# 1/sigma of a leaving chunk: from GpSimd's power to ScalarE's logarithm and exponential

## The chip, the cores and the metric

The kernel runs on one core of a Trainium2 chip. The metric is the device time of one execution in microseconds (us). A core has five engines with a queue each: TensorE (PE; its weight loads are shown apart as PEld), VectorE (DVE), ScalarE (ACT), GpSimd (POOL) and SyncE (SP), which here only issues transfers. SBUF is the memory on the core, PSUM the small memory that TensorE writes and that VectorE and ScalarE can read.

## The reference

Two layers on an image batch x of shape 8 x 128 x 128 x 128 (image, height, width, channel). Layer 0 is linear attention with a norm and a residual. Layer 1 is a selective scan over each image in four directions. What the change touches is the end of layer 1, for all 8 x 16384 tokens of 256 inner channels:

```python
y = (y0 + y1 + y2 + y3).transpose(0, 2, 1)      # the four scans' sums, one row a token
zf = jax.nn.silu(z.reshape(Bb, L, Cd))
yz = y * zf
mu = yz.mean(-1, keepdims=True)
xc = yz - mu
var = (xc * xc).mean(-1, keepdims=True)
yn = gamma * xc / jnp.sqrt(var + 1e-05) + beta
out = yn @ Wout
```

and each scan, for the step t of a direction, with the decay dA = exp(delta * A) and delta a softplus:

```python
xc = dA * xc + dut[..., None] * Bt[:, :, None, :]
y = jnp.einsum('kbcn,kbn->kbc', xc, Ct)
```

## The kernel before

The program has three stages one after the other: layer 0, the front of layer 1 (projection, 3x3 convolution, silu, and what the scans need, written to DRAM), and the scans with the end of layer 1 (`layer1_scan`). The change lies in the third, which begins at about 4436 us of the profiled execution.

The third stage holds y for one image in SBUF, as two tiles of 128 channels by 16384 positions. It goes through 8 output images o, four scans (slots) each, and every scan in 16 chunks of 1024 positions: 512 units, one in each call of `step(n)`. A chunk of a scan, for each half c of the channels:

- `load` (L923) and `load_rows` (L916, L917) bring the inputs through SP's queue; `delta` (L934, TensorE) and `soften` (L938, ScalarE's softplus into tile sp) make delta one step ahead;
- `decay` (L942, ScalarE) makes the decays with Exp, in PSUM (tile px);
- `weigh` (L951, GpSimd) multiplies sp with the input ubt into h, one of two buffers in turn;
- `scan` (L959 forward, L961 backward, VectorE) runs the recurrence over h, starting from the last column of the h of the chunk before;
- `emit` (L979, L982, L989 or L993, VectorE) multiplies with C, which `spread` (L967, TensorE) laid out; for the first slot of an image it writes y itself, for the others `gather` (L1001, VectorE) and `add` (L1009, GpSimd) add to y.

Softplus and Exp need different activation tables, so each step has two ACT_TABLE_LOADs, put there by the compiler ahead of the first activation that needs one.

When an image's four scans are done, its 16 chunks *leave* during the first 16 steps of the next image (for the last image, in 16 steps after all scans): `leaving[n]` is the chunk of step n. In `step`, `now` is the chunk that leaves in this step, `last` the one of the step before, `soon` the next. For a chunk m:

- `gate` (L1029) multiplies y with silu(z) into z: one half on GpSimd a step earlier, the other on VectorE; `square` (L1032, ScalarE) puts the squares into y;
- `moments` (L1042, TensorE) makes the mean and the mean of squares, `keep` (L1048, ScalarE) copies them, `to_tokens` (L1054, TensorE) turns them, `square_mean` (L1058, ScalarE, tile mv), `variance` (L1062, VectorE): rstd = mean of squares minus squared mean, 128 x 8 numbers, at the end of the step;
- `deviation` (L1066, L1067, GpSimd), one step later, between the two weighings: 1/sigma as (max(var, 0) + 1e-5) to the power -0.5, the exponents taken from the tile `half2`;
- `project` (L1074, TensorE) applies Wout, and `store` (L1080, VectorE), one step later between the two scans, multiplies with 1/sigma, adds a constant row and sends the tile r (two buffers) to DRAM.

`add_d` (L907, a DMA issue of GpSimd that adds the D term into y) stands at the end of some steps around an image's change, `fetch` (SP) brings z.

`in_order` ties every instruction of an engine to the one written before it on the same engine. So the order in `step` is the order of each queue; the engines run apart as far as their data lets them. `deviation(last[1])` stands after `weigh(n, 0)` in the text, hence in GpSimd's queue between the two weighings:

```python
        if last:
            deviation(last[1])
        if live:
            weigh(n, 1)
```

Of the kernel before, what the change touches and what calls it, by code (L numbers as in the profile page):

```python
# [8 lines left out]
F32 = mybir.dt.float32  # L9
BF16 = mybir.dt.bfloat16  # L10
AF = mybir.ActivationFunctionType
ALU = mybir.AluOpType
# [4 lines left out]
P = 128  # L17
# [7 lines left out]
GW = 4  # L25
# [9 lines left out]
EPS1 = 1e-5  # L35
# [712 lines left out]
def layer1_scan(ctx: ExitStack, tc, ubs, xps, zs, gs, dtw, dtb, a_log, gamma, beta, w_out, out):  # L748
# [15 lines left out]
    nc = tc.nc  # L764
    const = ctx.enter_context(tc.tile_pool(name="l2c", bufs=1))
# [31 lines left out]


    NR = R + 2
    half = const.tile([P, GW, 2], F32, name="half2")  # L800
    nc.vector.memset(half, -0.5)
    rws, dws = [], []
    for i in range(3):
        t = const.tile([P, CH], BF16, name=f"rows{i}")
# [104 lines left out]
    def load_rows(n):  # L909
        sl, i = units[n]  # L910
        m = sl.at(i)
        rw = rws[n % 3]
        md = NCH - 1 - m if sl.dt_turned_back else m
        src = xps[sl.dt_image, sl.dt_order].rearrange("j r l -> (j r) l")
        for j in range(3):
            nc.sync.dma_start(rw[3 * NR * j : 3 * NR * j + 3 * NR, :], src[:, md * CH : md * CH + CH])  # L916
        nc.sync.dma_start(rw[96:99, :], xps[sl.b, sl.order, :, R + 1, m * CH : m * CH + CH])  # L917

    def load(n, c):
        sl, i = units[n]  # L920
        m = sl.at(i)
        ubt[n, c] = wp.tile([P, CH], F32, name="ubt", tag="ub", bufs=4)
        nc.sync.dma_start(ubt[n, c], ubs[sl.b, sl.order, c][:, m * CH : m * CH + CH])  # L923
# [16 lines left out]
    def decay(n, c):  # L940
        sl, i = units[n]
        nc.scalar.activation(da[n, c], sp[n, c], AF.Exp, scale=sa[:, sl.s, c : c + 1])  # L942

    def weigh(n, c):
        if c == 0:
            hs[n] = wp.tile([P, NC2, CH], F32, name="h", bufs=2)
        u, t, h = ubt.pop((n, c)), sp.pop((n, c)), hs[n][:, c, :]
        if units[n][0].permuted:
            u = u.rearrange("p (e h w) -> p h e w", e=2, w=W // 2)
            t, h = (v.rearrange("p (h e w) -> p h e w", e=2, w=W // 2) for v in (t, h))  # L950
        nc.gpsimd.tensor_tensor(h, u, t, ALU.mult)  # L951

    def scan(n, c):
        sl, i = units[n]
        x, e = da[n, c], hs[n][:, c, :]
        last = 0 if sl.back else CH - 1
        start = 0.0 if i == 0 else hs[n - 1][:, c, last : last + 1]
        if sl.back:
            nc.vector.tensor_tensor_scan(e[:, ::-1], x[:, ::-1], e[:, ::-1], start, ALU.mult, ALU.add)  # L959
        else:  # L960
            nc.vector.tensor_tensor_scan(e, x, e, start, ALU.mult, ALU.add)  # L961
# [7 lines left out]
    def emit(n, hf):  # L969

        sl, i = units[n]
        h = hs[n][:, :, hf * 512 : hf * 512 + 512]
        c = cps.pop((n, hf)).to_broadcast([P, NC2, GN])
        if sl.place == 0:
            v = sl.y_at(i, hf)
            split = "p c (a b) -> p c a b"
            nc.vector.tensor_tensor(v, h.rearrange(split, b=H), c.rearrange(split, b=H), ALU.mult)  # L979
            return  # L980
        if hf != sl.first:
            nc.vector.tensor_tensor(h, h, c, ALU.mult)  # L982
            return
        p = da.pop((n, 1))
        if sl.y_turned:
            ts[n] = p.rearrange("p (c b a) -> p c b a", c=NC2, a=GW)
            t = p.rearrange("p (c b a) -> p c a b", c=NC2, a=GW)
            split = "p c (a b) -> p c a b"
            nc.vector.tensor_tensor(t, h.rearrange(split, b=H), c.rearrange(split, b=H), ALU.mult)  # L989
        else:  # L990
            t = p.rearrange("p (c q) -> p c q", c=NC2)
            ts[n] = t.rearrange("p c (a b) -> p c a b", b=H)
            nc.vector.tensor_tensor(t, h, c, ALU.mult)  # L993

    def gather(n):

        sl, i = units[n]
        v = sl.y_at(i, sl.first)
        if sl.y_turned:
            v = v.rearrange("p c a b -> p c b a")  # L1000
        nc.vector.tensor_tensor(v, v, ts.pop(n), ALU.add)  # L1001
# [15 lines left out]
    def mirrored(o, m, hf):  # L1017
        p = 2 * m + hf
        return 2 * NCH - 1 - p if o % 2 == 1 else p

    def fetch(o, m):
        for hf in range(2):
            zt[m, hf] = z = wp.tile([P, NC2, GN], F32, name="z", bufs=6)
            p = mirrored(o, m, hf)
            nc.sync.dma_start(z, zs[o].rearrange("c p l -> p c l")[:, :, p * GN : p * GN + GN])

    def gate(o, m, hf, eng):
        z, ym = zt[m, hf], piece(m, hf)
        eng.tensor_tensor(z, ym[:, :, ::-1] if o % 2 == 1 else ym, z, ALU.mult)  # L1029

    def square(m, hf):
        nc.scalar.activation(piece(m, hf), zt[m, hf], AF.Square)  # L1032

    def moments(m):

        pm = pe.tile([P, GN], F32, name="pm", tag="pt")
        for c in range(NC2):
            for j in range(2):
                for hf in range(2):
                    at = 32 * (2 * j + hf)  # L1040
                    v = piece(m, hf) if j else zt[m, hf]
                    nc.tensor.matmul(pm[at : at + 32, :], mean, v[:, c, :], start=(c == 0), stop=(c == NC2 - 1))  # L1042
        pts[m, "rows"] = pm
# [16 lines left out]
    def variance(m):  # L1060
        rst[m] = rstd = sm.tile([P, GW, NC2], F32, name="rstd")
        nc.vector.tensor_tensor(rstd, pts.pop(m)[:, :, :, 1], mv.pop(m), ALU.subtract)  # L1062

    def deviation(m):
        rstd = rst[m]
        nc.gpsimd.tensor_scalar(rstd, rstd, 0.0, EPS1, ALU.max, ALU.add)  # L1066
        nc.gpsimd.tensor_tensor(rstd, rstd, half, ALU.pow)  # L1067

    def project(m, hf, bank):
        z = zt.pop((m, hf))  # L1070
# [36 lines left out]
    def step(n):  # L1107
        live = 0 <= n < N
        then = n + 1 < N
        before = 1 <= n <= N  # L1110
        now, last, soon, later = (leaving.get(n + i) for i in (0, -1, 1, 2))
        first = before and units[n - 1][0].place == 0
        if before:
            half1 = units[n - 1][0].first
            emit(n - 1, half1)
            if not first:
                gather(n - 1)
        if now and last:
            gate(*now, 1, nc.vector)
        if before:  # L1120
            emit(n - 1, 1 - half1)
        if n + 2 < N:
            load_rows(n + 2)
        if n in fetched:
            fetch(*fetched[n])
        if live:
            decay(n, 0)
        if now:
            square(now[1], 1)
        if live:  # L1130
            decay(n, 1)
            weigh(n, 0)
            if n + 2 < N:
                load(n + 2, 0)
        if last:
            deviation(last[1])
        if live:
            weigh(n, 1)
            if n + 2 < N:
                load(n + 2, 1)  # L1140
        if now:
            moments(now[1])
        if live:
            scan(n, 0)
            da.pop((n, 0))
        if last:
            for hf in range(2):
                store(*last, hf)
        if then:
            for c in range(NC2):  # L1150
                delta(n + 1, c)
        if now:
            keep(now[1])
        if then:
            soften(n + 1, 0)
        if now:
            to_tokens(now[1])
            square_mean(now[1])
        if then:
            soften(n + 1, 1)  # L1160
        if live:
            scan(n, 1)
        if first:
            hs.pop(n - 1)
        if now:
            variance(now[1])
        if live:
            half1 = units[n][0].first
            spread(n, half1, "pc")
            spread(n, 1 - half1, "pt")  # L1170
        if soon and now:
            gate(*soon, 0, nc.gpsimd)
        elif soon:
            gate(*soon, 1, nc.gpsimd)
        elif later:
            gate(*later, 0, nc.gpsimd)
        if soon:
            square(soon[1], 0)
        if now:
            p = da.pop((n, 1)) if live else px.tile([P, CH], F32, name="px")  # L1180
            for hf in range(2):
                project(now[1], hf, p[:, hf * 512 : hf * 512 + 512])
        elif live and units[n][0].place == 0:
            da.pop((n, 1))
        if before and not first:
            add(n - 1)
            hs.pop(n - 1)
        if n in weighed:
            units[weighed[n]][0].weights()
        if n in summed:  # L1190
            add_d(*summed[n])
# [78 lines left out]
```

## Time and profile before

| | |
|---|---|
| median of 3 runs | 9188.95 us (9188.0 to 9196.81) |
| profiled execution, its own time | 9184.71 us |
| its span, first to last instruction | 9182.9 us |
| mean granted TensorE clock | 0.797 |
| GpSimd: clamp L1066, 128 x | 143.7 us, mean 1123 ns |
| GpSimd: power L1067, 128 x | 212.6 us, mean 1661 ns |
| GpSimd: weighing L951, 1024 x | 2420.9 us, mean 2397 ns |
| VectorE: gate L1029, 120 x | 261.3 us, mean 2177 ns |
| VectorE: variance L1062, 128 x | 18.1 us, mean 142 ns |
| ScalarE: table loads at L938 and L942, 512 x each | 656.9 us each, mean 1283 ns |
| ScalarE: square of the mean L1058, 128 x | 22.6 us, mean 177 ns |

Of the profile, the page gives the busy time of each engine in 40 slices of the span, as digits in tenths; a timeline lists one engine's instructions with start and length in us from the span's start, and in brackets the idle time before an instruction with the work that seems to have ended it; `x2` joins equal neighbours. A waits view lists who waited for whom. Recorded lengths include time in which an instruction had started and could not go on.

### The profile page before, as it was taken

To read this page: it belongs to the slowest core of one execution; us is meant where nothing else is said; L and a number is where in the kernel's file an instruction comes from. 1 tells how busy PE (TensorE), PEld (TensorE's weight loads), DVE (VectorE), ACT (ScalarE), POOL (GpSimd) and SP (SyncE) were. 2 spreads that over 40 slices of the span, in tenths; PEclk is the share of its full clock that TensorE was granted. 3 is DMA by queue.
4 is the path that set the end of the run, shared out by engine and by line. 5 is a ranking of instruction groups with operands and counts; after the bars stand their busy time and mean duration, and the time that the engine had idled before them with its cause. 6 is when DMAs were issued, how large, how long until landed. Compare 5 with 4: busy or idle time off the path is not lost. (4 is left out here: it accounts for less than half of the span.)

```text
span 9182.9 us, 91090 instructions
## 1 busy us (share of the span) xinstructions
PE 6273.2 (68%) x24350; PEld 3080.2 (34%) x24512; DVE 7929.7 (86%) x7889; ACT 7102.3 (77%) x8066; POOL 7317.2 (80%) x4684
## 2 busy tenths in 40 slices
PE   8999999998899999999334536345363463643636
PEld 5556555564333333333102304023041130311403
DVE  6667666673899999999799999999999999999996
ACT  5565665568799999999687887888888878788885
POOL 3446544465689988888599898998999989999897
PEclk9999999999999999999556758557575575755857
DMA  1322333313488888888659668586685876958767
GB/s 77 147 103 86 136 117 147 147 54 150 167 244 252 249 246 245 242 245 242 197 161 245 195 194 249 155 246 205 188 258 154 233 213 179 259 162 219 231 175 213
DMA packets 934769, 1750.66 MB, mean 191 GB/s; under 512 B 150228, under 2 KB 376148, under 8 KB 926064
## 3 DMA queue, kind: packets, MB, share of 16 engines
q1 hardware_dynamic: 873328, 1509.92, 49.9%
q0 software_dynamic: 60928, 234.90, 13.9%
q8 instruction: 200, 3.28, 0.1%
q14 instruction: 313, 2.56, 0.1%
HBM read 1052.36 MB, written 692.12 MB: 190 GB/s over the span
## 5 line engine op out<-in xcount | busy, mean ns | idle before, releaser
L951 POOL TENSOR_TENSOR h<-ubt,sp 128x1024 f32<-128x1024 f32 x1024 | 2420.9, 2397 | 342.5 <-ACT mv L1058 118.1
L934 PE MATMUL px<-rows,dtw 128*128 128x512 bf16 x1893 | 909.9, 573 | 2302.7 <-DVE y L1001 1084.5
L534 DVE SCALAR_TENSOR_TENSOR acc<-xb,cw,acc 128x1024 f32<-128x1024 f32 x1024 | 1320.5, 1290 | 133.0 <-ACT xb L502 89.5
L526 POOL TENSOR_TENSOR tap<-tap 128x1024 f32<-128x1024 f32 x512 | 1223.2, 2392 | 245.3 <-ACT tap L524 221.6
L938 ACT ACTIVATE sp<-px 128x1024 f32<-128x1024 f32 x1024 | 1046.6, 1023 | 435.6 <-PE px L934 391.4
L934 PEld LDWEIGHTS <-dtw 128*128 128x128 bf16 x2048 | 168.8, 110 | 3093.0 <-issue 1027.2
L961 DVE TENSOR_TENSOR_SCAN h<-px,h 128x1024 f32<-128x1024 f32 x512 | 1177.5, 2332 | 32.3 <-ACT px L942 15.9
L959 DVE TENSOR_TENSOR_SCAN h<-px,h 128x1024 f32<-128x1024 f32 x512 | 1178.0, 2331 | 21.0 <-POOL h L951 18.7
L1009 POOL TENSOR_TENSOR y<-y,h 128x512 f32<-128x512 f32 x768 | 1162.8, 1561 | 3.0 <-DVE h L982 3.0
L942 ACT ACTIVATE px<-sp,sa 128x1024 f32<-128x1024 f32 x1024 | 1110.4, 1109 | 6.1
L515 PE MATMUL acc<-xi,wt 128*128 128x512 f32 x2048 | 938.6, 601 | 53.7 <-ACT ures L539 53.5
L524 ACT ACTIVATE tap<-xb,cw 128x1024 f32<-128x1024 f32 x768 | 837.4, 1139 | 15.0 <-POOL xb L499 14.8
L282 POOL TENSOR_TENSOR q<-q,qs 128x512 f32<-128x512 f32 x256 | 273.0, 1066 | 694.6 <-DVE qs L281 691.1
L938 ACT ACT_TABLE_LOAD x512 | 656.9, 1283 | 169.5 <-PE px L934 122.8
L942 ACT ACT_TABLE_LOAD x512 | 656.9, 1283 | 9.2
L1074 PEld LDWEIGHTS px<-wg,z 128*128 128x128 f32 x4096 | 566.4, 222 | 114.9 <-issue 109.1
L967 PE MATMUL pc<-rows,csel 128*128 128x512 bf16 x1017 | 515.4, 588 | 85.1 <-DVE rstd L1062 76.2
L515 PEld LDWEIGHTS acc<-xi,wt 128*128 128x128 f32 x2048 | 375.9, 190 | 573.9 <-issue 412.9
L1074 PE MATMUL px<-wg,z 128*128 128x128 f32 x4096 | 565.5, 305 | 0.0
L488 PE MATMUL pxb<-xi,wi 128*128 128x512 f32 x1024 | 496.3, 607 | 2.1 <-ACT xb L497 2.1
L1001 DVE TENSOR_TENSOR y<-y,px 128x1024 f32<-128x1024 f32 x384 | 468.6, 1220 | 14.4
L982 DVE TENSOR_TENSOR h<-h,pc 128x1024 f32<-128x1024 f32 x384 | 466.0, 1214 | 0.0
(152 smaller groups left out, 14653.6 us busy)
## 6 DMA issues: line engine op xcount, KB each, us to landing
ubt<-ubs SPq DMA_DIRECT2D x1024, 512.0 KB
zs<-z SPq DMA_DIRECT2D x512, 256.0 KB
ubs<-ures SPq DMA_DIRECT2D x256, 512.0 KB
ubs<-turned SPq DMA_DIRECT2D x256, 512.0 KB
z<-zs SPq DMA_DIRECT2D x256, 512.0 KB
y<-gs POOLq DMA_DIRECT2D x128, 1024.0 KB, 10.2
gs<-du POOLq DMA_DIRECT2D x96, 1024.0 KB, 8.8
rows<-xps SPq DMA_DIRECT2D x1536, 60.0 KB
```

The costliest lines, as they stand in the source:

```text
L515: nc.tensor.matmul(acc[:, s, :], wt[:, j, c, :], x, start=(j == 0), stop=(j == len(ON_PE) - 1))
L524: nc.scalar.activation(t, at(n, c, *d), AF.Copy, scale=weight(n, c, *d))
L526: nc.gpsimd.tensor_tensor(sums[n, c], sums[n, c], t, ALU.add)
L534: nc.vector.scalar_tensor_tensor(acc, at(n, c, *d), weight(n, c, *d), acc, ALU.mult, ALU.add)
L934: nc.tensor.matmul(p[:, hf * 512 : hf * 512 + 512], sl.dw[:, c * P : c * P + P], src, start=True, stop=True)
L938: nc.scalar.activation(t, da[n, c], AF.Softplus)
L942: nc.scalar.activation(da[n, c], sp[n, c], AF.Exp, scale=sa[:, sl.s, c : c + 1])
L951: nc.gpsimd.tensor_tensor(h, u, t, ALU.mult)
L959: nc.vector.tensor_tensor_scan(e[:, ::-1], x[:, ::-1], e[:, ::-1], start, ALU.mult, ALU.add)
L961: nc.vector.tensor_tensor_scan(e, x, e, start, ALU.mult, ALU.add)
L1009: nc.gpsimd.tensor_tensor(v[:, c], v[:, c], h[:, c], ALU.add)
L1074: nc.tensor.matmul(po[:, w, :], z[:, c, w * H : w * H + H], wg[:, c, :], start=(c == 0), stop=(c == NC2 - 1))
```

## The change

1/sigma is made in three instructions on two other engines. VectorE clamps the variance and adds epsilon right behind `variance`, at the end of the step in which the chunk leaves. ScalarE takes the logarithm and then exp(-0.5 x) of it in the next step, after both decays and the square, ahead of the weighing in the text. GpSimd's two instructions go, and the tile of exponents `half2` with its memset. At the head of such a step, before the first decay, the activation table set `natural_log_exp_and_others` is asked for by name: a set that serves both Ln and Exp, so that the decays' Exp and the two new activations can run from it.

```diff
     NR = R + 2
-    half = const.tile([P, GW, 2], F32, name="half2")
-    nc.vector.memset(half, -0.5)
...
     def variance(m):
         rst[m] = rstd = sm.tile([P, GW, NC2], F32, name="rstd")
         nc.vector.tensor_tensor(rstd, pts.pop(m)[:, :, :, 1], mv.pop(m), ALU.subtract)
+        nc.vector.tensor_scalar(rstd, rstd, 0.0, EPS1, ALU.max, ALU.add)

     def deviation(m):
         rstd = rst[m]
-        nc.gpsimd.tensor_scalar(rstd, rstd, 0.0, EPS1, ALU.max, ALU.add)
-        nc.gpsimd.tensor_tensor(rstd, rstd, half, ALU.pow)
+        nc.scalar.activation(rstd, rstd, AF.Ln)
+        nc.scalar.activation(rstd, rstd, AF.Exp, scale=-0.5)
...
         if n in fetched:
             fetch(*fetched[n])
+        if last:
+            nc.scalar.preload_act_table_set("natural_log_exp_and_others")
         if live:
             decay(n, 0)
         if now:
             square(now[1], 1)
         if live:
             decay(n, 1)
+        if last:
+            deviation(last[1])
+        if live:
             weigh(n, 0)
             if n + 2 < N:
                 load(n + 2, 0)
-        if last:
-            deviation(last[1])
         if live:
             weigh(n, 1)
             if n + 2 < N:
```

## The prediction

> **What bounds the kernel now.** I read the page first, then the timeline of one engine at a time over one step of the scans, then the waits, then single lines where two engines meet.
>
> The page says that from slice 17 on VectorE and GpSimd are both almost full, and ScalarE is not:
>
> ```profile
> PE 6273.2 (68%) x24350; PEld 3080.2 (34%) x24512; DVE 7929.7 (86%) x7889; ACT 7102.3 (77%) x8066; POOL 7317.2 (80%) x4684
> ...
> DVE  6667666673899999999799999999999999999996
> ACT  5565665568799999999687887888888878788885
> POOL 3446544465689988888599898998999989999897
> ```
>
> That share doesn't say what GpSimd's part is worth where the change acts: in the 128 steps in which a chunk leaves. Three timelines (start, length, engine, line) of one such step, from one variance (L1062) to the next 11.28 us later, show it.
>
> ```profile
> 5064.44 0.13 DVE L1062 TENSOR_TENSOR rstd<-pq,mv 128x8 f32<-128x8 f32 x1
> 5064.62 1.22 DVE L979 TENSOR_TENSOR y<-h,pc 128x1024 f32<-128x1024 f32 x1
> 5065.76 2.34 DVE L1029 TENSOR_TENSOR z<-y,z 128x1024 f32<-128x1024 f32 x1
> 5068.02 1.21 DVE L979 TENSOR_TENSOR y<-h,pc 128x1024 f32<-128x1024 f32 x1
> 5069.15 2.34 DVE L959 TENSOR_TENSOR_SCAN h<-px,h 128x1024 f32<-128x1024 f32 x1
> ```
>
> ```profile
> 5064.65 2.37 POOL L951 TENSOR_TENSOR h<-ubt,sp 128x1024 f32<-128x1024 f32 x1 [1.33 <-ACT mv L1058]
> 5066.98 1.23 POOL L1066 TENSOR_SCALAR rstd<-rstd 128x8 f32<-128x8 f32 x1
> 5068.29 1.66 POOL L1067 TENSOR_TENSOR rstd<-rstd,half 128x8 f32<-128x8 f32 x1
> 5069.91 2.37 POOL L951 TENSOR_TENSOR h<-ubt,sp 128x1024 f32<-128x1024 f32 x1
> ```
>
> ```profile
> 5066.06 1.28 ACT L942 ACT_TABLE_LOAD   x1
> 5067.35 1.12 ACT L942 ACTIVATE px<-sp,sa 128x1024 f32<-128x1024 f32 x1
> 5068.41 1.04 ACT L1032 ACTIVATE y<-z 128x1024 f32<-128x1024 f32 x1
> 5069.35 1.10 ACT L942 ACTIVATE px<-sp,sa 128x1024 f32<-128x1024 f32 x1
> 5071.44 0.58 ACT L1048 COPY sr<-pm 128x512 f32<-128x512 f32 x1 [0.99 <-PE pm L1042]
> ```
>
> See three things. First, GpSimd sits idle 1.33 us before its first weighing (L951); that starts 0.14 us after the second scan (L959, 5062.18 + 2.33) ends, because the new h goes into a buffer that this scan still reads. The name L1058 in the bracket can't be the cause, it ended 0.7 us earlier. Second, VectorE's gate (L1029) takes 2.34 us here and 1.22 us at the end of the program, where GpSimd is idle:
>
> ```profile
> 9065.93 1.22 DVE L1029 TENSOR_TENSOR z<-y,z 128x1024 f32<-128x1024 f32 x1
> ```
>
> It does not run at half speed: it stands until the weighing ends (5064.65 + 2.37 = 5067.02) and needs 1.08 us from there. GpSimd's small clamp (L1066), queued behind the weighing, ends only with the gate. The two engines exclude one another, and a whole GpSimd instruction has to finish first. Third, the step is a closed chain: weighing 0.21 us after the variance starts, 2.37, gate 1.08, then by start times L979 1.05, scan 2.26, store (L1080) 2.05, scan 2.26; together 11.28. The deviation (L1066, L1067) is not in it.
>
> **The change part by part.** *GpSimd loses* L1066 and L1067: 143.7 + 212.6 = 356 us over 128 steps. They are off the chain above, so in an ordinary step their removal is worth nothing. What hides them is the idle 1.33 us and the fact that the second weighing, ended at 5072.3, is wanted only at 5073.46; it will start about 1.8 us earlier and GpSimd will only idle longer.
>
> *ScalarE gains* a logarithm and an exponential on 128x8. The nearest rows are 177 ns (L1058) and 208 ns (L778); with some 0.1 us between dependent ones, 0.5 us a step. They stand after the second decay (ends 5070.45) and before L1048, where ScalarE waits 0.99 us for TensorE. They'd be done at about 5071.0, the store needs 1/sigma at 5071.41. Cost 0, with 0.4 us of cover; if that were gone the store would pay the overrun. The clamp is long finished by then.
>
> *The table.* The load before L942 stays one load; it only names a set with both functions, and Square and Copy run under every table in this trace. Softplus takes it away again as now. Cost 0. The row gives 1.28 us for a load and the next activation follows at once (5066.06 to 5067.35), so two loads too many would take 2.6 us of ScalarE a step. The Trainium skill, "ScalarE: Activation LUTs", section "What ACT_TABLE_LOAD costs", adds a drain of 1.38 us to each switch, 2.66 us in all. By that page two loads too many would be 5.3 us, an estimate; the row has no such drain. In the last 16 steps, where no scan runs, the load may be repeated 16 times: 1.28 us inside ScalarE's pauses before the second Square; 0 to 4 us in all, I take 0.
>
> *VectorE gains* the clamp, 128x8 from and to SBUF. Bare, it is near L210 (214 ns) or L1062 (132 to 167 ns). Even 0.2 us on VectorE is hidden in an ordinary step, since the gate behind it waits 1.26 us for the weighing anyway. What counts is who gets in first, because this form also waits for GpSimd. The only row of the same shape shows it: the clamp-like L779 stood 1.00 us until a GpSimd fill was over.
>
> ```profile
> 4436.51 1.00 DVE L779 TENSOR_SCALAR sa<-sa 128x8 f32<-128x8 f32 x1
> ```
>
> ```profile
> 4436.09 1.40 POOL L805 MEMSET rows<- 128x1024 bf16 x1
> ```
>
> The Trainium skill speaks against the change here: "GPSIMD Engine Reference", section "8. Key points", says that GpSimd shares its SBUF interfaces with VectorE, which collides in a two-port mode or with two SBUF inputs. By that page alone, as an estimate, each of the 112 clamps beside a scan could be made to wait.
>
> Who waits is settled by start times. In an ordinary step the weighing starts 0.208 to 0.226 us after the variance does. The clamp depends on the variance's end (0.132) and dependent VectorE instructions follow 35 ns after the one before (L210, L212 and L281 show 34 to 36 ns idle), so it starts at 0.167, some 42 ns ahead. The closest meetings in the trace: a copy that started with a GpSimd product (333.62) won and delayed it by 0.6 us; a copy 42 ns behind one (910.84 against 910.80) lost and took 1.56.
>
> ```profile
> 333.62 0.73 DVE L152 COPY v<-x 128x512 f32<-128x512 f32 x1
> ```
>
> ```profile
> 910.84 1.56 DVE L152 COPY v<-x 128x512 f32<-128x512 f32 x1
> ```
>
> So I take it that the clamp wins, with 0 to 0.06 us delay for the weighing (gates let GpSimd go about 0.13 us before their recorded end; the clamp's end at 0.3 to 0.38 then gives 0.17 to 0.25 against 0.21).
>
> I went through all 112 variances that lie beside scans. 93 are ordinary: 93 x 0.02 = +2 us (0 to 6).
>
> 12 are late: the variance waited for ScalarE's L1058 by about 0.55 us after a store held by its buffer, and the weighing was already running. There the clamp stands to its end, L979 follows, the second weighing, no longer behind the deviation, enters before the gate, and the gate waits again. At 5613.91: weighing ends 1.94 after the variance, second 4.30, gate 5.39, next variance 13.0 instead of 11.26: +1.76. Twelve make 21 us; but VectorE's waits for the store buffer in these stretches are 20.1 us, and a delay just before such a wait is taken out of it. The late ones come in runs with these waits between them, so I keep 9 us (0 to 21).
>
> 7 are the first of an image, with GpSimd in an add (L1009). Where it lasts 1.5 to 2.1 us more (5 cases) the clamp waits it out and the weighing passes the gate, but the scan's wait of 1.13 us for the late weighing goes: +1.27 each. In the other 2, +0.1. Sum +6.6 us. Against it, GpSimd was late in the step after (add, deviation and DMA issue L907 in one step: 12.3 us, five times, and 11.7 twice, against 11.28); without the deviation it isn't: 5 x 1.03 + 2 x 0.39 = -5.9 us. L907's issue moves up some 2 to 3 us, as do the loads of ubt on SP's queue that wait for the second weighing; nothing is queued behind them that VectorE misses.
>
> The end (16 steps of 7.34 us, TensorE products and ScalarE copies in turn): the clamp delays the gate by 0.2 us against about 1 us of cover. 0. The removed memset, once, is 0.06 us before the loop.
>
> Sum: 2 + 9 + 6.6 - 5.9 = +11.7 us on the profiled execution (9184.71, its span 9182.9); that execution lies 4.24 us under the median 9188.95. I predict 9188.95 + 11, about 9200.
>
> **The rivals.** *The weighing wins* (slower). If the clamp starts only some 50 to 85 ns later than reckoned, each ordinary step goes like a late one: weighing ends 2.57, L979, second weighing 4.92, gate 6.0, next variance 13.63: +2.35, 93 times, 219 us, with the rest about 9420. For it: the margin is 42 ns, and after a scan L979 follows only at 0.105 us, as it waits for two things. Against: the clamp waits for one.
>
> *The second weighing passes the gate* even when the clamp won, being ready at once: about +2.3 us a step, 9425. Against it: wherever a waiting VectorE instruction met the end of a GpSimd one, it got in, as the gate above did.
>
> *Relief* (faster). The seven stretches of leaving chunks have 37 us beyond 15 steps of 11.28 each, mostly store waits. If an earlier L907 and earlier loads untangle the transfers and the late steps vanish, up to -37: some 9160. Against: the amount of data is the same.
>
> *The merging fails:* a load for the decays and one for the logarithm; first decay 1.28 later, 1/sigma at about 5073.4 instead of 5071.41: +2.0 x 112, 9413. Nothing in the profile speaks for it but that the trace has no such set.
>
> **How the numbers follow.** Likeliest case 0.57, its own range 9180 to 9220 (terms at their ends, and 10 us for shifted transfers); weighing wins 0.20; second weighing 0.05; relief 0.13; tables 0.04; the remaining 0.01 slower. This kernel can be told from no change at about 0.2%, 18 us. Inside the likeliest, 0.39 fall within that and 0.18 above. Faster 0.13; same 0.39; slower 0.18 + 0.20 + 0.05 + 0.04 + 0.01 = 0.48. To leave out no more than 2 in 10 the range must reach the lost race: 9165 to 9440, which leaves out about half of relief and the far ends.
>
> **What would show it.** Right: clamps of 0.13 to 0.3 us in 93 steps, steps of 11.3 us, GpSimd's idle before L951 up by some 2.9 us, clamps near 2 us in the late and first steps, 1024 loads before L938 and L942 or in their place plus at most 16. Wrong: clamps of 2.4 us everywhere with steps of 13.6; store waits gone; more loads. The whole stands on 35 ns between dependent VectorE instructions and on start times being the order of entry.

## The result, and the profile after

| | before | after |
|---|---|---|
| median, side by side | 9193.18 us (9188.0 to 9198.33, 6 runs) | 9229.87 us (9218.37 to 9244.15, 6 runs) |
| ratio | | 1.0042, 95% interval 1.0029 to 1.0054 |
| profiled execution, its span | 9182.9 us | 9242.3 us |

The changed kernel is slower by 37 us, 0.4%. The forecast was 9200 us, +11. Its times also spread over 26 us where those of before spread over 10, and the execution that was profiled is the slowest of its six (9244.15 us). Of the experiments' executions two, of `e5` and `e6`, ran at 11954 and 14046 us with a granted clock of 0.54 and 0.56; they are slow ones and left out of the ratios.

The line of busy time and the costliest group on GpSimd, from the page of the changed kernel. Line numbers have moved by one to two: L949 is the weighing, L1060 the variance, L1061 the new clamp, L977 emit, L1027 the gate, L1079 the store.

```profile
PE 6335.4 (69%) x24512; PEld 3079.4 (33%) x24512; DVE 8013.9 (87%) x8016; ACT 7168.9 (78%) x8338; POOL 7063.2 (76%) x4428
...
L949 POOL TENSOR_TENSOR h<-ubt,sp 128x1024 f32<-128x1024 f32 x1024 | 2485.5, 2465 | 620.2 <-ACT mv L1056 320.2
```

GpSimd lost 254 us of busy time. That is less than the 356 us of its two instructions, because records include waiting: those of the weighing grew by 65 us (2485.5 against 2420.9) and those of its gates by 29. It stands idle before the weighing for 620 us instead of 343. VectorE gained 84 us. The groups of VectorE by line (busy us, mean ns of one, idle before) show where:

```profile
L1061 DVE TENSOR_SCALAR rstd<-rstd 128x8 f32<-128x8 f32 x128 | 95.4, 746 | 4.4
L1060 DVE TENSOR_TENSOR rstd<-pq,mv 128x8 f32<-128x8 f32 x128 | 18.6, 146 | 30.6 <-ACT mv L1056 29.7
```

The variance before it, of the same shape, takes 146 ns; the clamp 746 on average. The view of this one line says that the average describes none of them (shortest, median and longest, in ns):

```profile
L1061 DVE TENSOR_SCALAR rstd<-rstd x128: 171/172/2357, 4980.4 to 9233.6; 128x8 f32<-128x8 f32 x128
```

**An ordinary step** goes as forecast. VectorE's timeline of the changed kernel, and GpSimd's for the same stretch:

```profile
8685.15 0.13 DVE L1060 TENSOR_TENSOR rstd<-pq,mv 128x8 f32<-128x8 f32 x1
8685.32 0.17 DVE L1061 TENSOR_SCALAR rstd<-rstd 128x8 f32<-128x8 f32 x1
8685.40 1.21 DVE L977 TENSOR_TENSOR y<-h,pc 128x1024 f32<-128x1024 f32 x1
8686.53 2.28 DVE L1027 TENSOR_TENSOR z<-y,z 128x1024 f32<-128x1024 f32 x1
```

```profile
8685.36 5.69 POOL L949 TENSOR_TENSOR h<-ubt,sp 128x1024 f32<-128x1024 f32 x2 [3.27 <-ACT mv L1056]
8691.01 2.36 POOL L1027 TENSOR_TENSOR z<-y,z 128x1024 f32<-128x1024 f32 x1
```

The clamp starts 0.17 us after the variance, 0.04 us ahead of the weighing, and is done in 0.17 us. GpSimd was idle for 3.27 us instead of 1.33; the prediction had put the rise at 2.9, and the rest of it stands in the record of the second weighing, which waits for the gate. The next variance comes at 8696.43, 11.28 us later. (`x2` joins the two weighings; VectorE's gate gets in between them.)

**A lost step** of the same image, 90 us earlier:

```profile
8594.75 0.17 DVE L1060 TENSOR_TENSOR rstd<-pq,mv 128x8 f32<-128x8 f32 x1
8594.96 2.21 DVE L1061 TENSOR_SCALAR rstd<-rstd 128x8 f32<-128x8 f32 x1
8597.08 1.21 DVE L977 TENSOR_TENSOR y<-h,pc 128x1024 f32<-128x1024 f32 x1
8598.22 2.33 DVE L1027 TENSOR_TENSOR z<-y,z 128x1024 f32<-128x1024 f32 x1
...
8608.38 0.17 DVE L1060 TENSOR_TENSOR rstd<-pq,mv 128x8 f32<-128x8 f32 x1
```

```profile
8594.78 4.67 POOL L949 TENSOR_TENSOR h<-ubt,sp 128x1024 f32<-128x1024 f32 x2 [5.61 <-ACT mv L1056]
8599.43 3.35 POOL L1027 TENSOR_TENSOR z<-y,z 128x1024 f32<-128x1024 f32 x1
```

The weighing starts 0.18 us ahead of the clamp. The clamp stands until it ends (8597.14), both weighings run back to back (4.67 us instead of 5.69), the gate waits for the second, and the next variance comes after 13.63 us. This is the course that the rival "the weighing wins" worked out, and it occurs in some steps only. That the length agrees to the hundredth is in part chance: the gate ends 5.80 us after the variance, not 6.0, and the next variance starts about as much later, since it waits for the mean (below).

Which steps? The lengths of the clamps of all 112 chunks that leave beside scans, read off the trace, show it: in the first and the seventh image the first eleven clamps are blocked (2.16 to 2.36 us), in the other five images the first one and one or two more, 34 in all. So most of the profiled execution's loss sits in two images. From an image's first variance to its sixteenth, beyond 15 steps of 11.28 us, in us:

| image | 1 | 2 | 3 | 4 | 5 | 6 | 7 | sum |
|---|---|---|---|---|---|---|---|---|
| before | 5.2 | 7.2 | 3.4 | 5.5 | 9.6 | 4.8 | 1.2 | 36.9 |
| after | 25.6 | 8.5 | 4.9 | 5.2 | 9.6 | 10.7 | 25.5 | 90.0 |

These stretches hold 53 of the 59 us by which the two spans differ, and images 1 and 7 alone 45. Some 4 us lie between the stretches and 3 in the last 16 steps.

**Why a run of lost steps keeps itself going.** TensorE's timeline in the lost step, then the same products in the ordinary step:

```profile
8595.19 3.73 PE L1073 MATMUL px<-wg,z 128*128 128x128 f32 x32
8601.82 1.07 PE L1040 MATMUL pm<-z,mean 128*32 128x512 f32 x2 [2.90 <-DVE y L977]
```

```profile
8690.08 0.62 PE L1040 MATMUL pm<-z,mean 128*32 128x512 f32 x2 [0.80 <-DVE y L977]
```

As emit and gate are late, TensorE pauses 2.90 us before the moments instead of 0.80, and then makes them at 1.07 us each instead of 0.62. The table by stretches (us, busy time of PE, PEld, DVE, ACT, POOL, then the granted clock, DMA share, GB/s) shows why:

```profile
8598.11:8601.51 3.40, 0.81 (x8) 0.62 (x6) 3.40 (x3) 1.83 (x2) 3.40 (x2) 1.00 0.73 211
8601.52:8604.92 3.40, 3.10 (x16) 1.02 (x16) 3.40 (x7) 1.46 (x4) 1.26 (x1) 0.50 0.90 310
8604.94:8615.16 10.22, 6.48 (x50) 5.12 (x46) 10.05 (x11) 8.21 (x10) 6.78 (x3) 1.00 0.57 172
8615.18:8618.58 3.40, 3.16 (x16) 1.01 (x16) 3.40 (x7) 1.40 (x4) 1.19 (x1) 0.50 1.00 320
```

In the interval with the pause TensorE is busy for 0.81 of 3.40 us; in the next one its granted clock is one half, and that one holds most of the moments. ScalarE's copy and softplus come later for it, and the square of the mean with them:

```profile
8608.17 0.17 ACT L1056 ACTIVATE mv<-pq 128x8 f32<-128x8 f32 x1
```

It starts at 8608.17 and ends at 8608.34, the last scan is over at 8608.24, and the next variance (8608.38) cannot start with the scan's end. In the ordinary step the same square is over 0.53 us before its variance (8685.15):

```profile
8684.44 0.18 ACT L1056 ACTIVATE mv<-pq 128x8 f32<-128x8 f32 x1 [0.48 <-PE pq L1052]
```

GpSimd's weighing doesn't need the mean, starts on time, and is first again. A variance that waits for the mean takes 0.17 us instead of 0.13, so the clamp is late by that too: it starts 0.20 us behind it, not 0.17. The five traces in which the clamp is on VectorE in SBUF and the mean is made at the same place (the changed kernel twice, `e4`, `e5`, `e10`) bear this out. First steps and steps with an added copy left aside, 92 clamps were blocked, and each of their variances began within 0.06 us of the end of the square of the mean; of the 426 that were not blocked, one did. Of the 91 steps examined (the first 13 of each image), the moments fall on a half-speed interval in 27: the first step of each image, as before the change, and the 20 steps that follow it in images 1 and 7 (in each the ten after the first).

### The profile page after: what moved, and what is told of

It is laid out like the page before. It is cut to its first block, busy times and chain, and to the rows that moved or that the text cites. A ratio compares the mean times of both kernels' runs of the same rounds, so it can differ in the third digit from the quotient of the medians.

```text
span 9242.3 us, 91051 instructions
## 1 busy us (share of the span) xinstructions
PE 6335.4 (69%) x24512; PEld 3079.4 (33%) x24512; DVE 8013.9 (87%) x8016; ACT 7168.9 (78%) x8338; POOL 7063.2 (76%) x4428
## 5 line engine op out<-in xcount | busy, mean ns | idle before, releaser
L949 POOL TENSOR_TENSOR h<-ubt,sp 128x1024 f32<-128x1024 f32 x1024 | 2485.5, 2465 | 620.2 <-ACT mv L1056 320.2
L932 PE MATMUL px<-rows,dtw 128*128 128x512 bf16 x2048 | 951.9, 564 | 2244.5 <-DVE y L999 1081.0
L936 ACT ACTIVATE sp<-px 128x1024 f32<-128x1024 f32 x1024 | 1047.2, 1024 | 434.0 <-PE px L932 413.6
L1007 POOL TENSOR_TENSOR y<-y,h 128x512 f32<-128x512 f32 x768 | 1159.2, 1556 | 4.8 <-DVE h L980 4.8
L940 ACT ACTIVATE px<-sp,sa 128x1024 f32<-128x1024 f32 x1024 | 1110.5, 1109 | 6.1
```

Of the source, the lines that this page charges most:

```text
L932: nc.tensor.matmul(p[:, hf * 512 : hf * 512 + 512], sl.dw[:, c * P : c * P + P], src, start=True, stop=True)
L936: nc.scalar.activation(t, da[n, c], AF.Softplus)
L1007: nc.gpsimd.tensor_tensor(v[:, c], v[:, c], h[:, c], ALU.add)
```

## The experiments

My theory from these traces: the ordinary step is won as predicted, the loss comes from clamps that lose their entry, and one loss makes the next. Rivals: ScalarE's part or its table costs something; GpSimd's earlier work disturbs the transfers. In the diffs lines are against the changed kernel where nothing else is said. Ratios stand against the kernel before on the same chip.

**Take the blocking away: the clamp reads PSUM.** The variance is written back to its PSUM tile.

```diff
-        nc.vector.tensor_tensor(rstd, pts.pop(m)[:, :, :, 1], mv.pop(m), ALU.subtract)
-        nc.vector.tensor_scalar(rstd, rstd, 0.0, EPS1, ALU.max, ALU.add)
+        v = pts.pop(m)[:, :, :, 1]
+        nc.vector.tensor_tensor(v, v, mv.pop(m), ALU.subtract)
+        nc.vector.tensor_scalar(rstd, v, 0.0, EPS1, ALU.max, ALU.add)
```

> The changed kernel, but the variance is written back into its PSUM tile and the clamp reads it there, so that the clamp no longer has both ends in SBUF; every instruction and its place in the queues stay. Theory (entry): the changed kernel loses because a clamp with both ends in SBUF has to wait for a GpSimd weighing that started before it, about 2.2 us each time, and the steps after a lost one lose again. Then here all clamps take 0.13 to 0.2 us, no step of 13.6 us is left, and the time is 9180 to 9195 beside 9193 for the kernel before. Rival (work): the added instructions themselves cost it; then the time stays near 9230. Rival (transfers): what GpSimd issues sooner crosses the stores; then also near 9230.

Measured: 9208.7 us (11 runs), ratio 1.0018 (1.0009 to 1.0027). The view of the clamp's line:

```profile
L1062 DVE TENSOR_SCALAR rstd<-pq x128: 166/166/168, 4977.9 to 9190.1; 128x8 f32<-128x8 f32 x128
```

Not one of 128 waits, late steps included, and no image loses step after step. 44 of them start and end while GpSimd is in an instruction. The expected time (9180 to 9195 us) was missed by 14 us all the same: something else costs. VectorE's waits for the store's buffer over the seven stretches and what lies between (4975 to 8760 us: total, times, longest) point to it. In order, they are before, in the changed kernel and here:

```profile
DVE r L1080 <- DMA out<-r: 20.1, 10, 3.4
```

```profile
DVE r L1079 <- DMA out<-r: 12.5, 9, 2.4
```

```profile
DVE r L1080 <- DMA out<-r: 38.3, 23, 3.9
```

In the changed kernel itself they are shorter than before. Where steps are made longer there is less to wait for: in `e3` below, where every step is lost, no such wait is left.

**No clamp on VectorE at all.** ScalarE does it as Relu, the epsilon goes in as the logarithm's bias.

```diff
-        nc.vector.tensor_scalar(rstd, rstd, 0.0, EPS1, ALU.max, ALU.add)
...
-        nc.scalar.activation(rstd, rstd, AF.Ln)
+        nc.scalar.activation(rstd, rstd, AF.Relu)
+        nc.scalar.activation(rstd, rstd, AF.Ln, bias=eps2[:, 0:1])
```

> The changed kernel with the clamp on ScalarE: a Relu ahead of the logarithm, epsilon as the logarithm's bias; VectorE has only the variance, as before the change. Entry: nothing of VectorE meets GpSimd but the gate; 9180 to 9195, ordinary steps of 11.28 us, the step after an image's first chunk down from 12.3 to 11.3. Rival (work on ScalarE: three small activations and the named table): above 9230. Rival (transfers): near 9230.

Measured: 9204.11 us (11 runs), ratio 1.0010 (1.0001 to 1.0018), 27.5 us of waits for the store's buffer. Nothing is blocked, and about 11 us (1 to 17 by the interval) are left that are no clamp's; 9180 to 9195 us had been expected.

**Put GpSimd's old work back.** The kernel of the last experiment, and GpSimd runs its old pair on a tile that nobody uses, between the weighings.

```diff
+        if last:
+            nc.gpsimd.tensor_scalar(old2, old2, 0.0, EPS1, ALU.max, ALU.add)
+            nc.gpsimd.tensor_tensor(old2, old2, half, ALU.pow)
         if live:
             weigh(n, 1)
```

> The kernel with the clamp on ScalarE, to which GpSimd's old clamp and power come back between the weighings, on a tile of their own that nobody else reads: GpSimd issues its adds of the D term when the kernel before does, and 1/sigma still comes from ScalarE. What is left over the kernel before with the clamp on ScalarE is 11 us (9204 against 9193), and VectorE's waits for a store buffer stand at 27.5 us against 20.1. Theory (transfers): GpSimd, 2.9 us sooner, sends the adds of the D term sooner into the stores; with its old timing the time is 9186 to 9198 and the store waits are near 20 us. Rival (work on ScalarE: three small activations a step make the rest): near 9204 still, store waits near 27.

Measured: 9196.31 us (11 runs), ratio 1.0000 (0.9991 to 1.0009). Waits for the store's buffer, with `e2` first and this one second:

```profile
DVE r L1081 <- DMA out<-r: 27.5, 21, 3.0
```

```profile
DVE r L1085 <- DMA out<-r: 19.3, 13, 3.0
```

So ScalarE's three activations and its table cost nothing that can be measured, and the rest of `e2` most likely comes with GpSimd's earlier second weighing. What follows that weighing and moves up with it are the loads of ubt and GpSimd's D-term transfers (L905); which of the two the stores collide with was not separated. The two ratios' intervals overlap (1.0001 to 1.0009), so the 11 us are uncertain by about as much. Nor do the two traces settle it: the profiled execution of `e2` is the fastest of its eleven (9192.81 us) and shorter than that of `e8` (9196.19), in spite of its longer waits.

**The clamp alone.** The kernel before, with the clamp moved to VectorE and the power left on GpSimd.

```diff
         nc.vector.tensor_tensor(rstd, pts.pop(m)[:, :, :, 1], mv.pop(m), ALU.subtract)
+        nc.vector.tensor_scalar(rstd, rstd, 0.0, EPS1, ALU.max, ALU.add)
...
-        nc.gpsimd.tensor_scalar(rstd, rstd, 0.0, EPS1, ALU.max, ALU.add)
         nc.gpsimd.tensor_tensor(rstd, rstd, half, ALU.pow)
```

> The kernel before with one part of the change: the clamp goes to VectorE behind the variance, the power stays on GpSimd between the weighings. Entry: clamps that start after a weighing wait for it as in the changed kernel; a lost step is a little shorter, since the power (1.66 us) and not the second weighing comes in before the gate: 9205 to 9240, with clamps of about 2 us in it. Rival (work on ScalarE) and rival (transfers): as before the change, 9190 to 9200, for ScalarE is untouched and GpSimd keeps its order.

Measured: 9211.8 us (10 runs), ratio 1.0015 (1.0006 to 1.0024), 22 clamps blocked, no run of lost steps: two in a row at most. A lost step here takes 12.2 us: the power still stands between the weighings, so the second weighing can't pass the gate. In image 4 every other step of the last eleven is lost, with the moments at full speed each time. The clamp on VectorE is enough to be slower; the power's removal makes each loss dearer.

**The clamp later.** One copy of a number per partition between variance and clamp.

```diff
+        nc.vector.tensor_copy(idle2, rstd[:, 0, 0:1])
         nc.vector.tensor_scalar(rstd, rstd, 0.0, EPS1, ALU.max, ALU.add)
```

> The changed kernel with one more VectorE instruction between variance and clamp, a copy of one number a partition into a tile that nobody reads. Entry: the clamp then starts some 0.1 us later, after the weighing (0.21 us behind the variance) in every step; all 112 clamps beside a scan take about 2.2 us, steps are 13.6 us, and the time is 9193 + 112 x 2.35 - 6, about 9450 (9420 to 9480). Rival (work): 128 instructions of 0.1 us more, about 9240. Rival (transfers): about 9230.

Measured: 9403.3 us (4 runs), ratio 1.0226 (1.0212 to 1.0240). A step that is otherwise ordinary, on VectorE and on GpSimd:

```profile
5783.85 0.13 DVE L1061 TENSOR_TENSOR rstd<-pq,mv 128x8 f32<-128x8 f32 x1
5784.02 0.15 DVE L1062 COPY idle<-rstd 128x1 f32<-128x1 f32 x1
5784.20 2.24 DVE L1063 TENSOR_SCALAR rstd<-rstd 128x8 f32<-128x8 f32 x1
```

```profile
5784.06 4.68 POOL L950 TENSOR_TENSOR h<-ubt,sp 128x1024 f32<-128x1024 f32 x2 [5.61 <-ACT mv L1057]
```

The clamp starts 0.14 us behind the weighing and all 112 lose. Start times do decide, and the size of the loss (210 us over 112 steps) is near the rival's 219 for 93, though below the 9420 to 9480 expected: the waits for the store's buffer, 20.1 us before, are gone. The 0.35 us of variance and copy are nothing beside it.

**Lose once.** The same copy, but in the seventh leaving step of each image only.

```diff
-            variance(now[1])
+            variance(now[1], kick=n % (K * NCH) == 6)
```

> The changed kernel with the extra copy between variance and clamp in a single step of each image, the seventh of its 16. Theory (a lost entry begets the next): behind the kicked step further steps are lost in at least some of the seven images, 9245 to 9330, and the profile has runs of clamps over 0.6 us that begin at the seventh step. Rival (each lost step for itself): seven lost steps more at 2.35 us, 9230 + 16 = 9246 at most, and the eighth step is ordinary again.

Measured: ratio 1.0061 (1.0044 to 1.0078). In images 2, 4 and 5 a run of lost steps was under way from the first step, before the copy came, and lasted to the tenth. In the other four images the copy's step was lost as well, but the moments of the next were made at full speed (2.0 us for all, against 3.5 us in the runs), and the next clamp won. In images 1 and 3 the step after that one was lost again, once, with the moments at full speed. So a lost step as such does not start a run, and my expectation of runs that begin at the copy fell; in every step of the runs the half-speed interval fell on the moments. The runs start in an image's first step. There GpSimd is in two adds (L1007), and where the second has not begun when the variance does, the clamp stands through the rest of the one and the whole of the other. In the four executions that leave this step alone (the changed kernel twice, `e4`, `e5`), 18 first clamps took up to 1.93 us and the next one won each time; 10 took 1.99 us or more and the next one lost each time. Why the border lies there is open.

**Make the mean sooner.** The copy, the turn and the square of the mean stand ahead of the next unit's delta and softplus.

```diff
         if then:
             for c in range(NC2):
                 delta(n + 1, c)
-        if now:
-            keep(now[1])
-        if then:
             soften(n + 1, 0)
-        if now:
-            to_tokens(now[1])
-            square_mean(now[1])
-        if then:
             soften(n + 1, 1)
```

(the three calls of the moved part now stand ahead of these lines)

> The changed kernel, but TensorE's turning of the means and ScalarE's square of the mean come ahead of the next unit's delta and softplus, so that the variance has its operands about 2 us sooner. Theory (a lost entry begets the next): in the runs of 13.6 us steps TensorE waits 2.9 us for the delayed emit, its clock falls for the moments, the square of the mean comes after the second scan's end, the variance and its clamp start late and the clamp loses again. With the mean sooner the runs of lost steps vanish: fewer than 20 clamps over 0.6 us (41 in the changed kernel), 9200 to 9220. Rival (each lost step is lost for itself, by the scan's end and the weighing alone): about 40 lost clamps, 9225 to 9240. A third way: softplus comes later and ScalarE holds the scans up, steps over 11.5 us without a lost clamp, above 9240.

Measured: 9257.63 us (5 runs), ratio 1.0068 (1.0055 to 1.0082). The runs are gone: all seven first clamps took 2.36 us or more, and all seven next ones won, though the moments between them were made mostly at half speed each time (3.3 to 3.7 us for all). That fits the theory but does not single out the mean, because the edit moved the weighing too. Softplus, which the weighing needs, now comes later. Here is the second leaving step of image 2, on VectorE and on GpSimd:

```profile
5585.14 0.13 DVE L1060 TENSOR_TENSOR rstd<-pq,mv 128x8 f32<-128x8 f32 x1
5585.31 0.17 DVE L1061 TENSOR_SCALAR rstd<-rstd 128x8 f32<-128x8 f32 x1
```

```profile
5587.08 5.21 POOL L949 TENSOR_TENSOR h<-ubt,sp 128x1024 f32<-128x1024 f32 x2 [3.87 <-ACT sp L936]
```

The weighing starts 1.94 us after the variance, and over all steps beside scans at least 0.47 us after it, instead of 0.21. With such a lead the clamp wins even where the mean is late: in two steps here it was, and neither clamp was blocked. Besides, the ordinary step is 11.8 us now, since the decays come late and the scans wait for them (70 us, against 4 before), which is the third way that was expected:

```profile
DVE h L957 <- ACT px L940: 37.0, 17, 2.6
DVE h L959 <- ACT px L940: 33.1, 15, 2.6
```

**Keep TensorE's clock up.** In the first leaving step the 16 products of the projection's second half are made twice, so TensorE is busy for some 1.8 us more in the pause (`project` runs its products `times` times).

```diff
-                project(now[1], hf, p[:, hf * 512 : hf * 512 + 512])
+                project(now[1], hf, p[:, hf * 512 : hf * 512 + 512], 1 + (live and hf == 1 and n % (K * NCH) == 0))
```

> The changed kernel, with the second half's 16 products of the projection done twice in the first leaving step of each image (the same numbers written twice, 1.9 us of TensorE in a pause of 2.9 us). If it is the half-speed clock after that pause that makes the next square of the mean late, and the lateness that loses the next clamp its entry, no image goes on losing after its first step: at most some 20 clamps blocked, no steps of 13.6 us in a row, image excesses of 5 to 11 us, 9200 to 9218 us, 15 to 25 us less than the changed kernel beside it. If the clock is only a symptom and the second weighing or the transfers keep the loss going, images still show ten lost steps in a row and the time is the changed kernel's.

Measured: 9226.76 us (6 runs), ratio 1.0034 (1.0021 to 1.0046). TensorE and then VectorE in the step after the longest first clamp:

```profile
4979.24 5.52 PE L1074 MATMUL px<-wg,z 128*128 128x128 f32 x48
4986.12 0.62 PE L1040 MATMUL pm<-z,mean 128*32 128x512 f32 x2 [1.36 <-DVE y L977]
```

```profile
4979.01 2.35 DVE L1061 TENSOR_SCALAR rstd<-rstd 128x8 f32<-128x8 f32 x1
...
4992.47 0.13 DVE L1060 TENSOR_TENSOR rstd<-pq,mv 128x8 f32<-128x8 f32 x1
4992.63 0.17 DVE L1061 TENSOR_SCALAR rstd<-rstd 128x8 f32<-128x8 f32 x1
```

A first clamp of 2.35 us, the moments at full speed, and the next clamp wins; without the extra products that came 0 times in 10. That this happened in one image only (the other six first clamps were short ones) is the weak side of it. No image loses more than single steps. The time is above what I expected: 30 us over before. If the doubled products cost nothing else, which was not tested, the runs are the smaller part of the median, and single losses and transfers the larger.

**The changed kernel again,** beside the last one.

> The changed kernel itself on the same chip, for comparison. Both theories: 9218 to 9245 us, with zero to three images losing ten steps in a row in the profiled execution.

Measured: 9237.25 us (4 runs, 9217.0 to 9256.09), ratio 1.0043 (1.0027 to 1.0060); in the profiled execution (9217.0) one image loses six steps in a row, the others one to three steps. The number of lost steps differs from execution to execution of one program, and with it the time. The interval overlaps that of `e10`, so the 10 us between them are not firm.

**Towards a faster version: both halves of the gate on GpSimd,** from the kernel of `e2`, since GpSimd now idles.

```diff
-        if now and last:
-            gate(*now, 1, nc.vector)
...
         if soon and now:
             gate(*soon, 0, nc.gpsimd)
+            gate(*soon, 1, nc.gpsimd)
```

> The kernel with the clamp on ScalarE, and VectorE's half of the gate goes to GpSimd too, behind the other half a step earlier, into the room that the deviation left. VectorE then never waits for GpSimd's port: its step is 0.18 + 2 x 1.14 + 2 x 2.26 + 2.05, some 9.0 us; GpSimd has 4 x 2.36 and a start of 0.2, 9.7 us; ScalarE about 10.3 us with its two table loads. Theory (entry; the gate's wait for the weighing and the weighing itself are on the chain): about 105 steps of 11.28 become 9.8 to 10.5 us, 9080 to 9150. Rival (transfers bind the leaving steps: DMA engines are 0.6 to 0.8 busy there): store waits take the gain, 9170 to 9200.

Measured: ratio 0.9997 (0.9987 to 1.0006); the gain expected did not come. The ordinary step is 10.8 us instead of 11.28, but the scans now wait for the decays (142 us), and the stores for their buffer:

```profile
DVE h L959 <- ACT px L942: 79.3, 56, 1.9
DVE h L961 <- ACT px L942: 62.2, 42, 3.8
DVE r L1081 <- DMA out<-r: 43.1, 18, 4.8
```

**The same, with ScalarE relieved:** the clamp from PSUM (lines as in the first experiment), and the copy of the moments on VectorE.

```diff
-        nc.scalar.copy(sr, pm)
+        nc.vector.tensor_copy(sr, pm)
```

> The changed kernel with the clamp reading PSUM, both halves of the gate on GpSimd, and the copy of the moments' sums (ScalarE's, 0.6 us) moved to VectorE behind the stores. With both halves on GpSimd and the clamp on ScalarE the ordinary leaving step was 10.8 us and the scans waited for the decays, 138 us over the leaving images. If ScalarE was what bound that kernel, taking 0.6 us of copy and 0.2 us of clamp off it per step shortens the ordinary step to 10.0 to 10.3 us: some 105 steps x 0.5 to 0.8 = 50 to 85 us less, 9105 to 9145 us. If the transfers of the stores bind instead (43 us of waits there), the step stays at 10.8 us and the time at 9180 to 9200 us, with store waits above 50 us.

Measured: 9244.6 us (4 runs), ratio 1.0053 (1.0036 to 1.0070); the ordinary step is 10.8 to 11.8 us. Both expectations fell. The last 16 steps, where the copy lies on the engine that ends them, became 21 us longer than in `e6` (137 to 158 us from the last scan on). ScalarE waits for TensorE's deltas instead (346 us ahead of the table load, 117 in `e6`). So ScalarE's load alone was not the bound. I take the step for a ring of TensorE, ScalarE and VectorE, in which work moved to one lengthens another part; no run shows that by itself. No version here beats the kernel before.

## Why the prediction was right or wrong

**Right: the order of entry in an ordinary step.** Clamp 0.163 to 0.175 us after the variance, weighing at 0.206 to 0.228, steps of 11.28 us; the +2 us forecast for delayed weighings do not show. `e3` shows how thin this is: one small instruction more and every step loses.

**Right: the price of a single loss.** A late step takes 13.0 us, as worked out at 5613.91, and a step lost otherwise takes 13.63, as the rival had it (13.60 in those steps of `e3` whose variance does not wait for the mean). "The weighing wins" was put at 9420; `e3` is that rival made real, at 9403.

**Right: ScalarE and its table at 0.** Table loads before L936 and L940 and by name are 512 + 400 + 128, that is 16 more than before, in the last steps. The logarithm takes 193 ns and the exponential 209. `e8`, with one activation more, gives the whole of it as 0 with an interval of 8 us to either side.

**Right in kind: relief after the first chunk.** In images 2 to 6 the first step is longer by 3.5 us in all, the second shorter by 3.0. At the forecast's prices these five come to 4.0 and 3.9.

**Wrong: the first steps, and the late steps' 9 us, as single events.** The prediction priced each lost entry once: +1.27 for five first steps, +0.1 for two, 9 us for twelve late ones. It had seen that late steps come in runs, but put that down to the stores and took it for a reason to discount. In three of its twelve late steps the weighing was not yet running; it started 0.15 to 0.18 us after the variance. A clamp loses there too, since it starts 0.20 us after a variance that waits, not the 0.167 reckoned. The +0.1 stood for first steps in which the second add had yet to begin when the variance did (0.13 and 0.24 us later, images 3 and 4 of the execution before). Just that position, in images 1 and 7 of the execution after (0.18 and 0.24 us), cost 20 and 24 us: the clamp does not get in between the adds but waits through both (2.19 and 2.25 us), TensorE pauses, its clock halves for the moments, the mean is late, the next clamp loses. The clock could be seen in the trace of before, where the moments of each image's first step are at half speed too; the prediction read no timeline and no clock of TensorE. Of this chain each link stands in the trace; by experiment only that of the clock was cut, in one image (`e10`).

**Probably wrong: the transfers at 0.** "Nothing is queued behind them that VectorE misses" fails by about 11 us (1 to 17): with no clamp on VectorE and nothing blocked (`e2`) the kernel is still slower than before, and not so when GpSimd's old work is back (`e8`). The stores' waits go the same way, 20 us, 27.5 and 19.3. The rival "relief" had the sign the other way round.

**The sum.** Of 37 us by medians, 21 (`e1`) to 26 (`e2`) are gone where no clamp is blocked. That is the firm part; the forecast had 9 + 6.6, about 16, for it. The other 11 to 15 stand against its 0 for the transfers and -5.9 for relief. A finer division is an estimate, as each of these differences is uncertain by about 10 us, and as the changed kernel's own store waits (12.5 us) don't show what `e2` loses. By it some 11 go to the transfers; what `e10` has beyond `e2`, some 19, to clamps blocked one at a time; and the remaining 7 to runs of lost steps (forecast 0). In the profiled execution the runs are far more, 45 of 59. The forecast had the sign of the sum and a third of its size. 9230 us lies above the likeliest case's own range (9180 to 9220); the whole range holds it because it was stretched to the rival in which nearly every step is lost, and that did not happen.

## What to carry to other kernels

- Where two engines exclude one another, a small instruction on the busy one costs a whole instruction of the other as soon as it comes second. Look at the distribution of its length, not at the mean, and ask what the loss does to the next round: a loss that makes its own cause late is not priced once.
- Work taken off an engine that has time to spare also moves what is queued behind it, its DMAs too. Here that probably cost about 11 us (`e2` against `e8`), where the work itself had cost nothing.
- A cheap cure for a blocked instruction is another place for its operand: from PSUM the same clamp never waited.

## What the runs showed of the hardware

**A source in PSUM is not held up.** The clamp on SBUF: 172 ns, or up to 2.36 us while GpSimd is in an instruction. From PSUM: 166 to 168 ns, 128 times, 44 of them with GpSimd in an instruction from start to end. The Trainium skill, "GPSIMD Engine Reference", section "8. Key points", names shared SBUF interfaces as the cause and a two-port mode or two SBUF inputs as the condition. The clamp has one SBUF input. That it runs in such a mode is not shown by these runs; that the source in SBUF is what exposes it to GpSimd is shown by `e1`.

**The clock's grid and the step.** In the trace's record of the granted clock of the changed kernel, all changes in these stretches lie on a grid of 3.413 us, with one half and full as the only values. In a run of lost steps every fourth interval is at half speed: they start at 8587.87, 8601.52, 8615.17, 8628.83 and 8642.48, each 13.65 us after the one before. Four intervals are 13.65 us and the lost step is 13.63, so the half-speed interval keeps falling on the moments, some 20 ns later each time. These two runs end after eleven steps (others after ten, six or two): the next half-speed interval then comes early and falls on the projection (8649.31 to 8652.71), and the moments are made at full speed:

```profile
8645.90:8649.30 3.40, 2.41 (x17) 1.40 (x14) 3.23 (x6) 3.06 (x5) 0.08 (x1) 1.00 0.66 260
8649.31:8652.71 3.40, 3.25 (x15) 3.16 (x15) 3.37 (x4) 3.37 (x4) 3.40 (x2) 0.50 0.17 42
8652.72:8662.95 10.23, 6.53 (x50) 4.17 (x50) 10.20 (x16) 7.15 (x11) 4.64 (x3) 1.00 0.79 239
```

The interval ahead of it holds 2.41 us of TensorE's work, the one in the lost step above held 0.81, and a half-speed one followed on both. How much work keeps the clock up is not worked out here.

The Trainium skill, "TensorE: Matmul & The Clock Gate", section "What's actually happening", gives the rule behind it: activity is judged in free-running windows of 3413 ns, and the clock is half or full. The trace agrees with both numbers. As such windows do not start with the program, where they lie against an image's first step would differ from execution to execution; that this is what makes the times of one kernel spread by 26 to 39 us here is likely, and was not tested. What was tested is only that the loss is not carried on where the moments are at full speed (`e10`, one image).
